# Adaptive layer norm, S4 convolution and a 2048x2048 FFN on one core: the first two row blocks convolved without their shift, and an impulse response from two frequency blocks

## The chip, the cores and the metric

The kernel runs on one core of one Trainium2 chip. The metric is the device time of one execution in microseconds (us), the median of several runs. The engines are TensorE (PE in the profile; PEld is its weight load), VectorE (DVE), ScalarE (ACT), GpSimd (POOL) and SyncE (SP); SP, and in a few places ScalarE, issue the DMA transfers.

## The reference, cut to what matters

The input `x` has 4 batches of 1024 rows with 2048 positions. A vector `c` per batch is multiplied with `wmod` and gives six modulation vectors for each batch: `sa, ca, ga` (shift, scale, gate) for the convolution, `sb, cb, gb` for the FFN.

```python
mod = (silu(c) @ wmod).reshape(4, 6, 1, -1)
h = layernorm(x) * (1 + ca) + sa
x = x + ga * s4(h)            # y = causal convolution of h with K along the row, + D*h
h = layernorm(x) * (1 + cb) + sb
x = x + gb * (h @ W.T + bias + low-rank update)
```

`K` is the impulse response of a state space model with 64 states: a rational function (`at_roots`) is evaluated at 2048 frequencies and brought back by an inverse Fourier transform. The convolution is linear: the convolution of `n*(1+ca) + sa` is that of `n*(1+ca)` plus that of `sa`, and the latter is one vector for all rows of a batch.

## The kernel before, in words

**Rows.** The 4096 rows are 32 row blocks of 128 ("row 0" to "row 31" below), eight to a batch. Each is a tile of 128x2048 f32.

**Modulation.** `wmod` is 100 MB of f32, read as six *sections* of 16 *chunks* of 1 MB each. `section` loads a chunk (`mod_load`, on SP's queue, L313) and multiplies it (`mod_mm`, L318: four matmuls with column tiling, each of two passes, so x8 in the trace) into one PSUM bank. The order is sections 1 (`ca`), 0 (`sa`), 2 (gate `ga`), 4, 3, 5. Sections 1 and 0 alternate between two pools of three chunk buffers each, later ones have three. After a section, `mod_column` copies the bank to `mrow`, transposes it (`mtp`) and keeps it as columns; `fold_scale` takes the largest value over the partitions (an all-reduce on GpSimd), makes a power of two of it and scales `ca` and `sa`. For section 2 `mod_gate` builds the gate on VectorE and ScalarE, and `gate_tile` spreads it over the partitions by four matmuls `gps` (L628) into `gat` (L629).

**Impulse response.** `toeplitz` is a generator; the list `KT` says after which chunks of sections 1 and 0 it goes a step further. `s4` spreads cosines and sines over the partitions by matmuls (`s4cs`, L153) for four blocks of 512 frequencies; both halves of the 128 partitions hold the 64 states (the lower half computes the real part, the upper the imaginary part). Each block takes some five elementwise steps of 128x512 and a reciprocal on VectorE (L163 to L171) and 4 matmuls `s4rp` (L178). Then follow small steps on 128x16, the transform (`s4kp`), the maximum, a store of the response to DRAM (`kd`, L257) and a load of it as 128 shifted copies (`kb`, L261, 1 MB, on ScalarE's queue). Four matmuls with an anti-diagonal matrix (`kbps`, L265) turn `kb` round, and VectorE makes six f16 filter tiles of it (`kh0..2`, `kl0..2`; high and low parts, L282 to L286).

**Convolution of a row.** `conv_load`, `stats` (L498 to L500), `normalize` (L515). `conv_prep` transposes the row in four groups of four (`tp`, L536, in two PSUM buffers of the pool `tps`), ScalarE applies scale and shift (`t`, L539), and both it and VectorE split the result in f16 halves (`hc`, `hs`, L545 to L548). `conv_mm` runs three families of f16 matmuls (L568) into the banks `ya` and `yb` of the pool `acc` (five banks, shared with `lps` and the FFN). Between the families it calls `tick`, which advances other work. ScalarE copies `ya` (`qs`, L581), VectorE adds `yb` to it (L585); with `early=False` VectorE also multiplies with the gate and adds `x` with row sums (L587 to L595). With `early=True`, for rows 0 and 1, that is left to `conv_late` (L604, L605), after the gate exists. `conv_post` stores the row to `x1d` and prepares the second layer norm; only after it can the buffer of `x` be loaded with the row four further on.

**Weights of the FFN.** From row 3 on (`R0`), `step` advances the generator `fill`: `prep_lora` loads `A` (`la`, L390) and `Bf` (`lb`, L403), both 2 MB in the same buffer (tag `we`), scales them, takes an all-reduced maximum and splits `lb` in `lbh` (ScalarE, L419) and `lbl` (VectorE, L420). `merge` then computes for eight column blocks products `lps` (L444, six matmuls to a PSUM bank) that VectorE adds to the weights `we` (L446), and stores the results. The rest of the time, after row 31, is the FFN itself (L704).

**Order.** The program is written in the order of `net`; a scheduler of the framework fixes the order of the instructions on each engine when the kernel is built, by data, buffers and priorities. On the chip each engine takes its list in that order. The names `s4cs`, `s4rp`, `kbps`, `tp`, `gps`, `lps` are tiles in the trace.

Of the kernel before, what the change touches and what calls it, by code (L numbers as in the profile page):

```python
# [24 lines left out]
P = 128  # L25
# [9 lines left out]
class Net:  # L35
# [40 lines left out]
    def s4(self, pool):  # L76
# [12 lines left out]
        cs = T([3, 2, D], "s4cs", BF16)  # L89
        nc.scalar.dma_start(out=cs, in_=io["t_cs"])  # L90
        one = T([3, P], "s4one", BF16)
        v.memset(one, 1.0)
# [30 lines left out]
        coef = T([P, 8], "s4coef")  # L123
        t8 = T([P, 8], "s4t8")
        lo, hi = slice(0, 64), slice(64, 128)
        lam, pv, qv, ct = (vec[:, i, :] for i in range(4))
        for i, (x, y) in enumerate(((ct, bq), (ct, pv), (qv, bq), (qv, pv))):
            re, im = t8[:, 2 * i : 2 * i + 1], t8[:, 2 * i + 1 : 2 * i + 2]
            tt(re, x[:, 0:1], y[:, 0:1], MUL)
            stt(re, x[:, 1:2], y[:, 1:2], re, MUL, ADD)  # L130
            tt(im, x[:, 1:2], y[:, 0:1], MUL)
            stt(im, x[:, 0:1], y[:, 1:2], im, MUL, SUB)
        t8v = t8.rearrange("p (v c) -> p v c", c=2)
        cov = coef.rearrange("p (v c) -> p v c", c=2)
        v.tensor_copy(coef[lo], t8[lo])
        tsc(cov[hi, :, 0], t8v[hi, :, 1], -1.0, None, MUL)
        v.tensor_copy(cov[hi, :, 1], t8v[hi, :, 0])
# [3 lines left out]
        fa = T([P, 2], "s4fa")  # L141
        v.tensor_copy(fa[lo, 0:1], nl[lo, 0:1])
        v.tensor_copy(fa[hi, 0:1], lam[hi, 1:2])
        v.memset(fa[lo, 1:2], 0.0)
        tsc(fa[hi, 1:2], ts2[hi], -1.0, None, MUL)
        rp = self.tps.tile([P, 16, 8], F32, tag="t", name="s4rp")
        w = 512
        cps = {}

        def table(c0):  # L150
            cps[c0] = [self.acc.tile([P, w], F32, tag="a", name="s4cs") for _ in range(2)]
            for i, ps in enumerate(cps[c0]):
                nc.tensor.matmul(ps, one, cs[:, i, ds(c0, w)], start=True, stop=True)  # L153

        yield
        table(0)
        table(w)
        for c0 in range(0, D, w):
            cc, sc = cps[c0]
            wi = pool.tile([P, w], F32, tag="s4wi", name="s4wi", bufs=2)  # L160
            wr = pool.tile([P, w], F32, tag="s4wr", name="s4wr", bufs=2)
            nu = pool.tile([P, w], F32, tag="s4nu", name="s4nu", bufs=2)
            tsc(wi, sc, ts2, None, MUL)  # L163
            stt(wi, cc, nl[:, 1:2], wi, MUL, ADD)
            nc.scalar.activation(wr, cc, AF.Square, scale=nl[:, 0:1])
            tsc(nu, sc, fa[:, 1:2], None, MUL)
            stt(nu, cc, fa[:, 0:1], nu, MUL, ADD)
            nc.scalar.activation(wi, wi, AF.Square)
            tt(wr, wr, wi, ADD)
            v.reciprocal(wr, wr)  # L170
            tt(nu, nu, wr, MUL)  # L171
            if c0 < 2 * w:
                yield
                table(c0 + 2 * w)
            yield
            for c in range(w // P):
                g = c0 // P + c
                nc.tensor.matmul(  # L178
                    rp[:, g, :], nu[:, ds(P * c, P)], coef,
                    start=(g == 0), stop=(g == NC - 1), skip_group_check=True,  # L180
                )
# [54 lines left out]
    def toeplitz(self, pool):  # L236
# [24 lines left out]
        nc.scalar.dma_start(out=kb, in_=src)  # L261
        yield
# [8 lines left out]
        self.kf = []  # L271
        for f in range(3):
# [5 lines left out]
            else:  # L278
                src = pool.tile([P, HC, P], F32, tag="kdif", name="kdif")
# [7 lines left out]
            self.kf.append((hi, lo))  # L287
# [77 lines left out]
    def fold_scale(self, pool, mul, add, name, winv=None):  # L365
# [9 lines left out]
        s, inv = self.pow2(self.cst, self.allmax(pool, m, NB, name), NB, name)  # L375
        for t in (mul, add):
            v.tensor_tensor(t, t, s.unsqueeze(1).to_broadcast([P, NC, NB]), MUL)  # L377
        return inv


    def prep_lora(self, pool, tmp):
# [21 lines left out]
        nc.sync.dma_start(out=b, in_=io["BfT"].rearrange("(k p) o -> p k o", p=P))  # L403
# [21 lines left out]
    def merge(self, pool, tmp, c):  # L425
        nc, v = self.nc, self.nc.vector
        lf = tmp.tile([P, 2, 2, P], F32, tag="laf", name="laf")
# [95 lines left out]
    def conv_prep(self, pl, r, x, st, out):  # L523
# [8 lines left out]
        for c0 in range(0, NC, 4):  # L532
# [4 lines left out]
            for k in range(4):  # L537
                c = c0 + k
                nc.scalar.activation(  # L539
                    t[:, k], tp[:, k], AF.Identity,  # L540
                    bias=self.sa[:, c, b : b + 1], scale=self.ca[:, c, b : b + 1],
                )
# [56 lines left out]
    def conv_late(self, x, y, sums):  # L599

        v = self.nc.vector
        for q in range(2):
            sl = ds(1024 * q, 1024)
            v.tensor_tensor(y[:, sl], y[:, sl], self.gat[:, sl], MUL)  # L604
# [164 lines left out]
WM, WMS = 3, 3  # L769
X0 = (20, 26)  # L770
LEFT0 = 30
KT = (0, 3, 5, 6, 8, 11, 14, 18, 24)
# [11 lines left out]
def net(ctx: ExitStack, tc: tile.TileContext, io):  # L784
# [40 lines left out]
    for name in ("lora", "mrg"):  # L825
        pl[name] = pool(right, "p1" + name, 1, "right")

# [12 lines left out]
    pl["sm"] = pool(left, "p1sm", 4)  # L840
    st = ExitStack()
    toe = k.toeplitz(pool(st, "st", 1))
    wms = pool(st, "wms", WMS)
# [3 lines left out]
    xs, hs = {}, {}  # L847
    sts = {}
    n = 0
    for sec in (1, 0):  # L850
        for _ in section(sec, (wms, wmp)):
            if n in KT:
                with tc.issue_after(k.last.ins), tc.high_priority():
                    take(toe, 1)
            if n in X0:
                r = X0.index(n)
                xs[r] = k.conv_load(pl, r)
# [209 lines left out]
```

## Time and profile before

| | us |
|---|---|
| median of 3 runs (2142.97 to 2143.06) | 2143.01 |
| the profiled execution | 2143.54 |
| its span, first to last instruction | 2141.7 |
| TensorE busy in the span | 2076.2 (97%) |
| VectorE, ScalarE busy | 1321.9 (62%), 928.7 (43%) |
| DMA moved | 483.06 MB, 226 GB/s on average |
| the two costliest groups: FFN matmuls L704 (5376), convolution matmuls L568 (3456) | 1198, 953 |

Mean granted clock of TensorE: 0.984 of full speed. In the profile a line is read as: place in the program, engine, operation, output tile from input tiles, shape, count, and in brackets the idle time of that engine just before it with the instruction or transfer that ended it. Matmuls are pipelined, so durations of single matmuls overlap; counts and start times are the better guide there.

### The profile page before, as it was taken

How to read it: one execution, taken by the hardware profiler on the slowest of the kernel's cores; microseconds unless marked ns; L12 is line 12 of the kernel's file. 1: busy time of each engine (PE TensorE's matmuls, PEld its weight loads, DVE VectorE, ACT ScalarE, POOL GpSimd, SP SyncE). 2: the span in 40 equal slices, each digit the busy share in tenths (PEclk: the TensorE clock that was granted, in tenths of full speed). 3: DMA queues.
4: the chain of work that ended last, by engine and by line, in shares of the span. 5: the costliest groups of instructions: out<-in, count | busy, mean ns of one | idle time of the engine just before them, and what ended most of it. 6: DMA issues, size and time to landing. Idle time of an engine off the chain costs nothing.

```text
span 2141.7 us, 28401 instructions
## 1 busy us (share of the span) xinstructions
PE 2076.2 (97%) x11084; PEld 1020.2 (48%) x11084; DVE 1321.9 (62%) x2357; ACT 928.7 (43%) x1699; POOL 3.3 (0%) x12
## 2 busy tenths in 40 slices
PE   7698999999999999999999999999999999999998
PEld 2144555455455555554545545545444444444444
DVE  7449889888899998665565565565533333332323
ACT  1148667666677766755454454555200000000000
POOL 0000000000000000000000000000000000000000
PEclk8799999999999999999999999999999999999999
DMA  9988578767875553387565565564794545455542
GB/s 401 377 297 312 190 295 300 269 245 274 315 297 180 185 190 117 133 347 262 182 241 187 194 228 193 203 236 176 272 354 160 189 155 171 163 162 168 175 158 70
DMA packets 127137, 483.06 MB, mean 226 GB/s; under 512 B 13670, under 2 KB 13799, under 8 KB 96023
## 3 DMA queue, kind: packets, MB, share of 16 engines
q1 hardware_dynamic: 126464, 479.65, 61.8%
q8 instruction: 87, 1.43, 0.3%
q10 hardware_dynamic: 538, 1.59, 0.2%
q14 instruction: 48, 0.39, 0.1%
HBM read 325.89 MB, written 155.30 MB: 225 GB/s over the span
## 4 chain that ended last, share of the span: by engine, by line
PE 73%; DVE 12%; ACT 5%; DMA 3%; issue 1%; SPq 0%; DVEq 0%; ACTq 0%
PE fZ L704 22%; PE fY L704 15%; PE fX L704 15%; PE ya L568 9%; PE yb L568 5%; PE tp L654 2%; PE lps L444 2%; PE modps L318 2%; DVE y L595 1%; ACT x L614 1%; ACT t L539 1%; PE tp L536 1%; DVE hc L548 1%; DVE st L498 1%; DVE y L594 1%
## 5 line engine op out<-in xcount | busy, mean ns | idle before, releaser
L704 PEld LDWEIGHTS <-lf 128*128 128x128 f16 x5376 | 526.0, 98 | 620.8 <-issue 1.1
L704 PE MATMUL fZ<-w,lf 128*128 128x512 f16 x2304 | 513.6, 379 | 0.8 <-ACT p L712 0.8
L704 PE MATMUL fX<-w,lf 128*128 128x512 f16 x1536 | 342.8, 379 | 0.0
L704 PE MATMUL fY<-w,lf 128*128 128x512 f16 x1536 | 342.0, 379 | 0.0
L568 PEld LDWEIGHTS <-hc 128*128 128x128 f16 x2304 | 214.5, 98 | 203.3 <-issue 40.6
L722 DVE TENSOR_TENSOR xo<-xo,gb 128x512 f32<-128x512 f32 x128 | 87.8, 690 | 241.8 <-DMA xo<-x1d 229.1
L539 ACT ACTIVATE t<-tp,sa,ca 128x128 f32<-128x128 f32 x512 | 202.5, 476 | 13.3 <-DVE sa L377 5.1
L568 PE MATMUL ya<-kh,hc 128*128 128x512 f16 (+3 forms) x768 | 191.7, 327 | 4.0 <-ACT qs L581 3.9
L568 PE MATMUL ya<-kh,hs 128*128 128x512 f16 (+3 forms) x768 | 194.1, 328 | 0.7 <-DVE hs L548 0.7
L568 PE MATMUL yb<-kh,hc 128*128 128x512 f16 (+3 forms) x768 | 190.9, 326 | 0.0
L712 ACT COPY p<-fZ 128x512 f32<-128x512 f32 x64 | 37.3, 583 | 285.6 <-PE fZ L704 271.9
L712 ACT COPY p<-fX 128x512 f32<-128x512 f32 x32 | 18.8, 587 | 316.3 <-PE fX L704 241.2
L568 PEld LDWEIGHTS <-hs 128*128 128x128 f16 x1152 | 107.7, 98 | 98.1 <-issue 18.3
L656 ACT ACTIVATE gt<-tp,sb,cb 128x256 f32<-128x256 f32 x256 | 125.6, 579 | 60.5 <-PE tp L654 60.5
L318 PE MATMUL modps<-wm,sct 128*32 128x512 f32 x768 | 121.6, 692 | 23.9 <-DMA wm<-in_wmod 15.3
L568 PE MATMUL ya<-kl,hs 128*128 128x512 f16 (+3 forms) x384 | 125.6, 327 | 0.0
L568 PE MATMUL ya<-kl,hc 128*128 128x512 f16 (+3 forms) x384 | 125.6, 327 | 0.0
L568 PE MATMUL yb<-kl,hc 128*128 128x512 f16 (+3 forms) x384 | 125.1, 326 | 0.0
L727 DVE TENSOR_TENSOR fin<-fX,gb 128x512 f32<-128x512 f32 x32 | 22.1, 692 | 128.2 <-PE fX L704 128.1
L536 PE MATMUL tp<-ident,n 128*128 128x128 f32 x512 | 80.6, 282 | 17.2 <-ACT t L539 13.8
L548 DVE TENSOR_TENSOR hc<-t,hc 128x512 f16<-128x512 f32 x128 | 87.6, 684 | 5.6 <-ACT hc L547 5.6
L444 PE MATMUL lps<-lbh,lac 128*128 128x512 f16 x256 | 85.0, 380 | 0.6 <-ACT lbh L419 0.6
(241 smaller groups left out, 2211.4 us busy)
## 6 DMA issues: line engine op xcount, KB each, us to landing
wm<-in_wmod SPq DMA_DIRECT2D x96, 1024.0 KB, 7.3
lfd<-lf SPq DMA_DIRECT2D x112, 512.0 KB, 3.2
lf<-lfd SPq DMA_DIRECT2D x112, 512.0 KB, 3.8
x<-in_x SPq DMA_DIRECT2D x32, 1024.0 KB, 5.6
x1d<-y SPq DMA_DIRECT2D x32, 1024.0 KB, 5.2
x<-x1d SPq DMA_DIRECT2D x32, 1024.0 KB, 5.6
xo<-x1d SPq DMA_DIRECT2D x128, 256.0 KB, 3.8
out<-xo SPq DMA_DIRECT2D x128, 256.0 KB, 3.3
```

What stands on the lines that cost most here:

```text
L318: self.last = self.nc.tensor.matmul(self.modps[32 * g : 32 * g + 32, :], self.sct[:, j].rearrange("p r b -> p (r b)"), w[:, ds(512 * g, 512)],
L444: nc.tensor.matmul(ps, la[:, x, k, h], y[:, k, osl], start=(n == 0), stop=(n == 5))
L536: nc.tensor.transpose(tp[:, k], n[:, ds(P * (c0 + k), P)], self.ident)
L539: nc.scalar.activation(t[:, k], tp[:, k], AF.Identity, bias=self.sa[:, c, b : b + 1], scale=self.ca[:, c, b : b + 1],)
L548: v.tensor_tensor(lo[:, sl], src, hi[:, sl], SUB)
L568: nc.tensor.matmul(pf[:, o:512], h, self.kf[f][z][:, ds(k0, 512 - o)], start=first, stop=(i == last and (x, z) == (1, 0)), skip_group_chec ...
L654: nc.tensor.transpose(tp[:, c, r], xs[r][:, ds(P * (c0 + c), P)], self.ident)
L656: nc.scalar.activation(t[:, c0 + c], tp[:, c], AF.Identity, bias=self.sb[:, c0 + c, b : b + 1], scale=self.cb[:, c0 + c, b : b + 1],)
L704: nc.tensor.matmul(ps[name], lf[i][:, k, x, :], wc[i][k // 4][:, k % 4, y, :], start=(first and n == 0), stop=(n == 3 * HC - 1), skip_grou ...
L712: nc.scalar.copy(t, ps[name])
L722: v.tensor_tensor(x, x, self.gbias[:, h], ADD)
L727: v.tensor_tensor(t, cv, self.gbt[:, h], MUL)
```

## The change

There are three parts.

1. *Impulse response.* The partitions' halves now hold the same states at different frequencies (0 to 1023 in the lower, 1024 to 2047 in the upper). The table has six rows in place of three, and the matrix that spreads it comes with it from DRAM. There are two blocks of 512 columns in place of four; the real and the imaginary part of each summand are both kept, and two `s4rp` matmuls per 128 columns, with coefficients that are zero for the other half, take the place of one. The six filters are made in the order 0, 2, 1, and `kb` is kept for `shift_conv`.
2. *Rows 0 and 1 without the shift.* `early_scale` makes a scale `es` from `ca` of batch 0 alone, when section 1 is done. Rows 0 and 1 are prepared with it and without `sa`, and convolved between the chunks of section 0 (`row` advances that section from `conv_mm`). When `sa` is known, `shift_conv` convolves it by 16 small f32 matmuls (`gsp`), and `shift_add` spreads the result over the partitions by 16 f32 matmuls (`gsb`) and adds it to both rows (eight adds on VectorE). `conv_late` multiplies these rows by the ratio of the two scales.
3. *The order around it.* Row 2 is convolved early as well (`EARLY = 3`), between section 2's chunks; the loop starts at row 3. The row pools are opened ahead of the impulse response, which with its chunk pool (two buffers, `WMS`) goes to the other side of the memory; the pools of `prep_lora` and `merge` are opened after it is closed. `lb` is loaded on ScalarE's queue; `laf` has two buffers.

The diff, cut to its core:

```diff
-        cs = T([3, 2, D], "s4cs", BF16)
-        nc.scalar.dma_start(out=cs, in_=io["t_cs"])
-        one = T([3, P], "s4one", BF16)
-        v.memset(one, 1.0)
+        ct = T([6, D + P], "s4cs", BF16)
+        nc.scalar.dma_start(out=ct, in_=io["t_cs"])
+        cs = ct[:, 0:D].rearrange("p (i n) -> p i n", i=2)
+        one = ct[:, D:]
...
-        def table(c0):
-            cps[c0] = [self.acc.tile([P, w], F32, tag="a", name="s4cs") for _ in range(2)]
-            for i, ps in enumerate(cps[c0]):
-                nc.tensor.matmul(ps, one, cs[:, i, ds(c0, w)], start=True, stop=True)
...
+        cps = [[self.acc.tile([P, w], F32, tag="a", name="s4cs") for _ in range(2)] for _ in range(2)]
+        for n in range(2):
+            for i, ps in enumerate(cps[n]):
+                nc.tensor.matmul(ps, one, cs[:, i, ds(n * w, w)], start=True, stop=True)
+
+        def tiles(name):
+            return [pool.tile([P, w], F32, tag=name, name=name, bufs=2) for _ in range(2)]
+
+
+        wi, wr = tiles("s4wi"), tiles("s4wr")
+        wq = pool.tile([P, 2, w], F32, tag="kdif", name="s4wq")
+        wq = [wq[:, n] for n in range(2)]
+        for n, (cc, sc) in enumerate(cps):
+            tsc(wi[n], sc, ts2, None, MUL)
+            stt(wi[n], cc, nl[:, 1:2], wi[n], MUL, ADD)
+            nc.scalar.activation(wr[n], cc, AF.Square, scale=nl[:, 0:1])
+            nc.scalar.activation(wq[n], wi[n], AF.Square)
+        for n, (cc, sc) in enumerate(cps):
+            tt(wq[n], wr[n], wq[n], ADD)
+            v.reciprocal(wq[n], wq[n])
+            stt(wr[n], cc, nl[:, 0:1], wq[n], MUL, MUL)
+            tt(wi[n], wi[n], wq[n], MUL)
             yield
             for c in range(w // P):
-                g = c0 // P + c
-                nc.tensor.matmul(
-                    rp[:, g, :], nu[:, ds(P * c, P)], coef,
-                    start=(g == 0), stop=(g == NC - 1), skip_group_check=True,
-                )
+                out = rp.rearrange("p (h g) v -> p g h v", h=2)[:, 4 * n + c]
+                for i, x in enumerate((wr[n], wi[n])):
+                    nc.tensor.matmul(
+                        out, x[:, ds(P * c, P)], cf[:, i],
+                        start=(n, c, i) == (0, 0, 0), stop=(n, c, i) == (1, 3, 1), skip_group_check=True,
+                    )
...
-        for f in range(3):
+        self.kf = {}
+        for f in (0, 2, 1):
...
-        s, inv = self.pow2(self.cst, self.allmax(pool, m, NB, name), NB, name)
+        self.hs, inv = s, _ = self.pow2(self.cst, self.allmax(pool, m, NB, name), NB, name)
...
+    def early_scale(self, pool):
+        v = self.nc.vector
+        m = pool.tile([P, 1], F32, tag="esm", name="esm")
+        v.tensor_reduce(m, self.ca[:, :, 0], AX.X, ALU.max, apply_absolute_value=True)
+        v.tensor_scalar(m, m, LNMAX, None, MUL)
+        self.es, self.einv = self.pow2(self.cst, self.allmax(pool, m, 1, "es"), 1, "es")
+        self.cae = self.kpool.tile([P, NC], F32, tag="cae", name="cae")
+        v.tensor_scalar(self.cae, self.ca[:, :, 0], self.es, None, MUL)
+
+    def shift_conv(self, pool):
+
+        nc, v = self.nc, self.nc.vector
+        sa = pool.tile([P, NC], F32, tag="sae", name="sae")
+        v.tensor_scalar(sa, self.sa[:, :, 0], self.es, self.hinv[:, 0:1], MUL, MUL)
+        ps = self.tps.tile([P, NC], F32, tag="t", name="gsp")
+        for m in range(NC):
+            nc.tensor.matmul(
+                ps[:, m:NC], self.kb[:, ds(P * m, P)], sa[:, 0 : NC - m],
+                start=(m == 0), stop=(m == NC - 1), skip_group_check=True,
+            )
+        self.gsc = self.kpool.tile([P, NC], F32, tag="gsc", name="gsc")
+        v.tensor_copy(self.gsc, ps)
+
+    def shift_add(self, ys):
+        nc, v = self.nc, self.nc.vector
+        for q in range(4):
+            ps = self.tps.tile([P, 4, P], F32, tag="t", name="gsb")
+            for c in range(4):
+                nc.tensor.matmul(
+                    ps[:, c], self.gsc[:, 4 * q + c : 4 * q + c + 1].to_broadcast([P, P]), self.ident,
+                    start=(c == 0), stop=(c == 3), skip_group_check=True,
+                )
+            for y in ys:
+                sl = ds(512 * q, 512)
+                v.tensor_tensor(y[:, sl], y[:, sl], ps.rearrange("p c t -> p (c t)"), ADD)
...
-        nc.sync.dma_start(out=b, in_=io["BfT"].rearrange("(k p) o -> p k o", p=P))
+        nc.scalar.dma_start(out=b, in_=io["BfT"].rearrange("(k p) o -> p k o", p=P))
...
-        lf = tmp.tile([P, 2, 2, P], F32, tag="laf", name="laf")
+        lf = tmp.tile([P, 2, 2, P], F32, tag="laf", name="laf", bufs=2)
...
+                if shift:
+                    nc.scalar.activation(
+                        t[:, k], tp[:, k], AF.Identity,
+                        bias=self.sa[:, c, b : b + 1], scale=self.ca[:, c, b : b + 1],
+                    )
+                else:
+                    nc.scalar.activation(t[:, k], tp[:, k], AF.Copy, scale=self.cae[:, c : c + 1])
...
-            v.tensor_tensor(y[:, sl], y[:, sl], self.gat[:, sl], MUL)
+            v.scalar_tensor_tensor(y[:, sl], y[:, sl], ratio, self.gat[:, sl], MUL, MUL)
...
-WM, WMS = 3, 3
-X0 = (20, 26)
+WM, WMS = 3, 2
+EARLY = 3
+X0 = 11
 LEFT0 = 30
-KT = (0, 3, 5, 6, 8, 11, 14, 18, 24)
+KT = (0, 5, 7, 11)
...
+    for name, bufs in (("h", 2), ("n", 1), ("t", 2), ("y", EARLY), ("g", 1)):
+        pl[name] = pool(left, "p1" + name, bufs)
     st = ExitStack()
-    toe = k.toeplitz(pool(st, "st", 1))
-    wms = pool(st, "wms", WMS)
+    toe = k.toeplitz(pool(st, "st", 1, "right"))
+    wms = pool(st, "wms", WMS, "right")
...
-    for sec in (1, 0):
-        for _ in section(sec, (wms, wmp)):
-            if n in KT:
-                with tc.issue_after(k.last.ins), tc.high_priority():
-                    take(toe, 1)
-            if n in X0:
-                r = X0.index(n)
-                xs[r] = k.conv_load(pl, r)
-                sts[r] = k.stats(pl, xs[r], "1")
-            n += 1
-    xs[2] = k.conv_load(pl, 2)
+    for _ in section(1, (wms, wmp)):
+        if n in KT:
+            with tc.issue_after(k.last.ins), tc.high_priority():
+                take(toe, 1)
+        if n == X0:
+            load(0)
+        n += 1
+    k.early_scale(msm)
+    load(1)
+    sec = section(0, (wms, wmp))
+    for r in range(2):
+        stats(r)
+        take(prep(r, False), 9)
+    take(sec, 1)
+    with tc.issue_after(k.last.ins), tc.high_priority():
+        take(toe, 2)
+    take(sec, 1)
+
+    def row():
+        take(sec, 1)
+
+    for r in range(2):
+        ys[r] = k.conv_mm(pl, hs.pop(r), xs[r], row, True)
+        load(r + 2)
+    take(sec, 17)
+    k.shift_conv(msm)
+    k.shift_add([ys[r][0] for r in range(2)])
     st.close()
...
+    for name in ("lora", "mrg"):
+        pl[name] = pool(right, "p1" + name, 1, "right")
...
     sec = section(2, (wmp,))
-    take(prep(0), 9)
-    take(prep(1), 9)
-    stats(2)
-    take(sec, 16)
-    load(3)
-    ys = {0: k.conv_mm(pl, hs.pop(0), xs[0], lambda: None, True)}
+    for r in range(2, EARLY + 1):
+        stats(r)
     take(prep(2), 9)
-    stats(3)
-    ys[1] = k.conv_mm(pl, hs.pop(1), xs[1], lambda: None, True)
+    ys[2] = k.conv_mm(pl, hs.pop(2), xs[2], row, True)
     nxt = prep(3)
+    take(nxt, 9)
+    take(sec, 17)
+    k.gat = k.gate_tile(pl["g"], 0)
+    ratio = k.kpool.tile([P, 1], F32, tag="rat", name="rat")
+    nc.vector.tensor_tensor(ratio, k.einv, k.hs[:, 0:1], MUL)
+    for r in range(EARLY):
+        k.conv_late(xs[r], *ys[r], ratio if r < 2 else 1.0)
+        k.conv_post(pl, r, xs.pop(r), *ys[r])
+        if r < 2:
+            load(r + 4)
+    stats(EARLY + 1)
+    nxt = prep(EARLY + 1)
     take(nxt, 1)
-    take(sec, 1)
-    k.gat = k.gate_tile(pl["g"], 0)
-    for r in range(2):
-        k.conv_late(xs[r], *ys[r])
-        k.conv_post(pl, r, xs.pop(r), *ys[r])
     post = None
-    for r in range(2, 32):
-        if r + 2 < 32:
+    for r in range(EARLY, 32):
+        if EARLY + 2 < r + 2 < 32:
```

## The prediction, made before the changed kernel ran

> **What bounds the kernel now.** I read the page first: TensorE (PE) has work for 97% of the span, so a gain must come from the 65 us in which it has none, or from the stretches in which it runs at a low clock. Then I asked for the busy time by stretch, cut where TensorE's behaviour changes; columns are busy us and instructions of each engine, granted TensorE clock, DMA share, GB/s.
>
> ```profile
> PE 2076.2 (97%) x11084; PEld 1020.2 (48%) x11084; DVE 1321.9 (62%) x2357; ACT 928.7 (43%) x1699; POOL 3.3 (0%) x12
> ```
>
> ```profile
> 8.59:97.70 89.11, 65.75 (x320) 18.69 (x321) 53.77 (x110) 8.88 (x15) 0.95 (x3) 0.74 1.01 421
> 97.70:105.50 7.80, 4.99 (x18) 1.78 (x16) 5.55 (x17) 4.45 (x12) 0.41 (x1) 0.72 0.45 188
> 105.50:162.50 57.00, 57.00 (x375) 24.95 (x373) 26.79 (x56) 27.83 (x71) 0.00 (x0) 1.00 0.85 294
> 162.50:207.50 45.00, 36.36 (x216) 19.15 (x214) 42.17 (x102) 40.18 (x69) 1.05 (x1) 0.93 0.85 330
> 207.50:300.00 92.50, 90.90 (x546) 47.02 (x545) 80.29 (x160) 63.05 (x132) 0.00 (x0) 1.00 0.65 245
> ```
>
> There are four regimes. Until 97.7 us the DMA is full (421 GB/s): the modulation weights of sections 1 and 0 set the pace, 2.49 us for each 1 MB chunk, and TensorE waits at clock 0.74. From 105.5 to 162.5 TensorE never stops (rows 0 and 1 with section 2's chunks). From 162.5 to 207.5 VectorE (DVE) is 94% busy and TensorE loses 8.6 us. After 207.5 TensorE is full again. So rows 0 and 1 can be moved into the first regime; the third is where it may be given back.
>
> The third regime in the timeline (start, duration, engine, line; in brackets idle time and what ended it). TensorE's rows first, then VectorE's:
>
> ```profile
> 196.83 1.09 PE L536 MATMUL tp<-ident,n 128*128 128x128 f32 x8 [1.56 <-DVE n L515]
> 199.18 0.66 PE L536 MATMUL tp<-ident,n 128*128 128x128 f32 x4 [1.26 <-ACT t L539]
> 201.41 1.12 PE L536 MATMUL tp<-ident,n 128*128 128x128 f32 x4 [1.57 <-ACT t L539]
> 204.58 1.91 PE L318 MATMUL modps<-wm,sct 128*32 128x512 f32 x2 [2.05 <-DMA wm<-in_wmod]
> 207.10 0.58 PE L444 MATMUL lps<-lbh,lac 128*128 128x512 f16 x1 [0.60 <-ACT lbh L419]
> 207.48 0.63 PE L568 MATMUL ya<-kh,hs 128*128 128x512 f16 x1
> ```
>
> ```profile
> 163.65 1.67 DVE L629 TENSOR_SCALAR gat<-gps,fs_i,ks_i 128x512 f32<-128x512 f32 x2 [0.80 <-PE gps L628]
> 165.35 1.23 DVE L604 TENSOR_TENSOR y<-y,gat 128x1024 f32<-128x1024 f32 x1
> 195.44 1.33 DVE L515 TENSOR_SCALAR n<-x,mv,rs 128x2048 f32<-128x2048 f32 x1
> ```
>
> The gate tile is there at 163.65; behind it on VectorE stand the late work of rows 0 and 1, and row 4's normalisation follows only at 195.44, 31.8 us later. TensorE lives meanwhile on the convolutions of rows 2 and 3 (35 us). Row 4's convolution starts at 207.5. I call this moment **row 4's entry** and compare the kernels there, since the work behind it is the same.
>
> **What the skill says.** "TensorE: Matmul & The Clock Gate", section "HAM oscillation — how this bites in real kernels", states that waits for DMA between short bursts throw the array back to half clock. The trace agrees: a chunk's eight matmul passes take 1.94 us in the first regime and 1.06 us from 107 us on. I use 1.94 until TensorE runs without pause and 1.06 after. "DMA: Bandwidth & Descriptors", section "Issuing engines are not separate DMA queues", says that a transfer issued by another engine shares the same DMA engines, so moving `lb` to ScalarE's queue buys no bandwidth; in the trace, `kb` on that queue needs 9.5 us for 1 MB while SP's weights stream.
>
> **Part 1, the impulse response.** Two frequency blocks in place of four: VectorE saves 2 x 3.34 us of reciprocals and two blocks of five or so 512-wide steps (0.65 to 0.75), 14 us. In the built order the last `s4rp` matmuls stand behind chunk 8, which arrives at 26 us: done at 28.3, plus 16 passes of 0.155 us (`s4rp` before: 8 in 1.24) makes 31 (before 48.5). From there 9.3 us to the store of `kd` (48.5 to 57.8 before) and 16.2 until `kb` lands (57.8 to 74.0): 57 us, 17 earlier.
> But `kbps` now stands behind other things on TensorE. The section 1 chunks end at 50.5 (chunk 12 at 36, then x0 and four chunks at 2.49, then 1.94); copy and transposes 2.1; the new early scale with its all-reduce 4.3 (`fold_scale`'s chain before takes 3.8, from 97.1 to 100.9); four `t` of ScalarE 1.6 that free the PSUM buffer; a transpose group 1.1; three quarters of a chunk 1.5: 61.2. Then 6.6 to the last copy of `kb` (73.97 to 80.57 before) and 10.1 for the six filters on VectorE (79.9 to 90.0): **TensorE runs without pause from 78 us**, with 21 chunks and 4.3 us of row 0 done, where before it did from 105.5.
>
> **Part 2, TensorE's work from 78 to the end of section 2.** A row is 41,472 columns at 0.216 us per 512: 17.5 us. Rest of rows 0 and 1 30.7, row 2 17.5, row 3's share in the built order 4.9; 27 chunks at 1.08 29.2; 48 transposes at 0.125 and the column's four 6.5; `shift_conv` 32 passes (between 0.13, the transposes, and 0.155, `s4rp`) 4.5; `shift_add` 32 passes at 0.13 4.1. Sum 97.4: 175.4. Waits in the built order: normalisation of row 1 0.5; gsp, copy, gsb, adds through two PSUM buffers 1.8 (eight adds at 0.6 on an idle VectorE); row 2's preparation now starts only after that, 1.5; row 3's transposes behind ScalarE 2; the last chunks through three buffers 1. I take 6.5 (3 to 12): **section 2 ends at 182** (154.4 before, but with a row and a half less behind it).
>
> **Part 3, the end of the early stage.** `prep_lora` is now followed closely. `la` is issued behind section 0 (117) and is harmless. ScalarE squares it within row 2's preparation and issues `lb` at about 152; 9.1 us to land (the row before; 5 to 19 by `kb` and `la`); scalings, row 3's preparation (11), the sums, the all-reduce and the second scaling put the first `lbh` at about 185 to 188. The first `lps` matmul, right behind section 2's last chunk, waits for it: 3 us (0 to 6), and row 3's convolution and the gate matmuls `gps` are queued behind that. The gate's absolute value on ScalarE also stands behind `lbh` (before at once, 155.2). With 7 us of matmuls and the two `lbl` of VectorE (2.25 each) between, **the gate tile starts at 192**.
> From there VectorE's built order to row 4's normalisation is: gate 3.2; 12 late steps for three rows at 1.15 (165.35 and on, start to start) 13.9; row 3's evacuation 3; six statistics 3.7; one `we` 0.7; two dozen small steps 2.9; the normalisation 1.3: 28.7. Transposes, `t`, casts 3: row 4's entry at **223.8**. In these 32 us TensorE has only 8.4 us of row 3, `gps` 2, four chunks 4.1 and 24 `lps` 5.2, the last behind PSUM banks that VectorE frees late.
>
> **The sum.** Before, entry at 207.5. Ahead of its entry the changed kernel has done 29 more `lps` (6.3), three quarters of a chunk more (0.8) and four transposes fewer (0.5): 6.6. So 223.8 - 207.5 - 6.6 = +9.7 us. The profiled execution took 2143.54 (span 2141.7 and 1.8 around it), 0.5 over the median of the runs: 2143.0 + 9.7 = **2152.7**. Hidden at no cost: the ratio in `conv_late` (same step), the f order, `laf`'s second buffer, two more x loads early (DMA is free after 78), s4's extra copies.
>
> **Rivals.** (1) *Faster, 2132.* Counted without VectorE's queue: TensorE starts 27.5 us earlier; since then it has extra 11 chunks 11.9, gsp and gsb 8.6, the column 0.5, minus 4.3 of row 0 and 0.2 transposes: 16.5. Gain 11, if its waits from there to 300 us stay at the 10.2 of before (8.6 and 1.6). For: in the first regime TensorE was idle or slow for over 40 us, and VectorE is nearly idle until 160. Against: three late rows hang on one gate, with one row to cover them in place of two. It decides from a gate tile at 182 or earlier. (2) *No change, 2143:* both halves meet; the gate at about 182 to 187, less idle behind it. (3) *Worse, 2161:* `lb` takes the 18 us of `la`, ScalarE waits with row 3's preparation behind it, +8. That the response isn't ready earlier (so the change misses its aim) ends here too: each us at 78 is a us at the end.
>
> **Numbers.** Forecast 0.53 (own range 2147.5 to 2158), rival 1 0.21, rival 2 0.14, rival 3 0.12. A measurement tells 0.2% (4.3 us) from no change: faster 0.21, same 0.14, slower 0.65. The range leaves out the outer halves of rivals 1 and 3 (0.17): 2131 to 2161.
>
> **What would show it.** In the profile after: `kb` landing near 57 and `kbps` near 61; PE share over 95% from 78 us; section 2's last chunk near 182; the first gate row on VectorE near 192; row 4's normalisation 27 to 30 us behind it, with TensorE idle for over 8 us just ahead, waiting on DVE `n` and `we`. I am wrong if the gate comes before 184, or if TensorE finds work in that stretch.

## The result, and the profile after

The changed kernel takes 2149.16 us (median of 8 runs, 2146.49 to 2152.91) beside 2142.84 (8 runs, 2141.51 to 2144.57) of the kernel before: ratio 1.003, interval 1.0019 to 1.004. It is 6 us slower. The profiled execution took 2149.26, its span 2147.5 (before 2143.54 and 2141.7).

First the line of busy time, from the page of the changed kernel:

```profile
PE 2085.0 (97%) x11144; PEld 1028.0 (48%) x11144; DVE 1313.8 (61%) x2356; ACT 922.0 (43%) x1697; POOL 3.0 (0%) x13
```

TensorE is busy 8.8 us longer and idle 3.0 us less (62.5 for 65.5): 5.8 us of span. Now the busy time by stretch of the changed kernel (columns as in the prediction):

```profile
8.59:50.00 41.41, 32.13 (x164) 11.57 (x160) 23.66 (x65) 2.30 (x4) 0.95 (x3) 0.75 0.99 405
...
60.00:69.00 9.00, 8.33 (x37) 2.85 (x32) 7.93 (x13) 6.53 (x20) 0.00 (x0) 1.00 0.97 403
69.00:130.00 61.00, 61.00 (x397) 29.80 (x394) 26.77 (x64) 13.52 (x36) 0.41 (x1) 0.97 0.77 293
130.00:180.00 50.00, 44.75 (x310) 19.83 (x302) 20.70 (x47) 33.32 (x71) 0.35 (x1) 1.00 0.84 321
180.00:200.00 20.00, 16.96 (x63) 5.70 (x60) 10.90 (x11) 8.57 (x6) 0.00 (x0) 0.75 0.80 290
200.00:230.00 30.00, 23.27 (x118) 10.26 (x117) 29.63 (x68) 12.71 (x26) 0.00 (x0) 0.83 0.87 330
230.00:300.00 70.00, 65.35 (x388) 33.55 (x387) 65.79 (x144) 54.13 (x115) 0.00 (x0) 0.98 0.70 250
```

The first regime ends at 69 us in place of 105.5: that is the aim of the change, and it is met. From 130 to 300 TensorE then loses 19.7 us, and from 180 to 230 its clock falls to 0.75 and 0.83 as well. The same stretches as single rows, TensorE's in the timeline of the changed kernel:

```profile
60.69 3.70 PE L263 MATMUL kbps<-kb,rev 128*128 128x512 f32 x8
68.65 0.38 PE L608 MATMUL ya<-kl,hs 128*128 128x512 f16 x1 [0.67 <-DVE kl L285]
...
185.70 0.58 PE L481 MATMUL lps<-lbh,lac 128*128 128x512 f16 x1 [2.10 <-ACT lbh L456]
...
213.03 0.38 PE L481 MATMUL lps<-lbh,lac 128*128 128x512 f16 x1 [2.54 <-DVE y L625]
...
218.45 0.59 PE L481 MATMUL lps<-lbh,lac 128*128 128x512 f16 x1 [3.35 <-DVE y L634]
...
227.52 0.38 PE L608 MATMUL ya<-kh,hs 128*128 128x512 f16 x1
```

And VectorE's, with the gate tile, the first late step and row 4's normalisation:

```profile
195.47 1.67 DVE L669 TENSOR_SCALAR gat<-gps,fs_i,ks_i 128x512 f32<-128x512 f32 x2 [3.90 <-PE gps L668]
197.18 1.28 DVE L644 SCALAR_TENSOR_TENSOR y<-y,rat,gat 128x1024 f32<-128x1024 f32 x1
...
222.04 1.33 DVE L552 TENSOR_SCALAR n<-x,mv,rs 128x2048 f32<-128x2048 f32 x1
```

The picture is the forecast one: the gate is late (195.5), row 4's normalisation is 26.6 us behind it, and the `lps` matmuls in between wait for PSUM banks that VectorE frees late (`y`). Row 4's convolution begins at 227.5.

**Where row 4 really begins in the kernel before.** The prediction took the `ya<-kh,hs` row at 207.48 for row 4. The convolution matmuls behind that point, and behind 228.10 (stretch, busy us and count, weight loads, clock, DMA share, GB/s):

```profile
207.40:2142.00 1934.60, 538.23 (x3096) 288.23 (x3095) 1.00 0.59 212
228.10:2142.00 1913.90, 524.45 (x3024) 281.37 (x3023) 1.00 0.60 213
```

28 rows of 108 are 3024. The 72 more belong to row 3: a row is worked in two halves of its output, the first of 36 matmuls and the second of 72, and 207.48 is the start of row 3's second half. Row 4 begins at 228.17. For the same reason the "rows 2 and 3 (35 us)" that the prediction has ahead of 207.48 are row 2 and a third of row 3 (144 matmuls, 23.7 us busy), and row 4's normalisation at 195.44 had 20.7 us of row 3 behind it as cover. From row 4's start to the first FFN matmul (L704, L744) the two kernels have nearly the same work. First the kernel before, its stretch and two groups of matmuls in it (count, busy us, mean ns, idle us just before):

```profile
228.10:920.25 692.15, 678.76 (x4210) 366.32 (x4208) 613.97 (x1277) 487.73 (x1008) 0.38 (x1) 1.00 0.63 234
```

```profile
L444 PE MATMUL lps<-lbh,lac 128*128 128x512 f16 x237 | 78.6, 379 | 0.0
L318 PE MATMUL modps<-wm,sct 128*32 128x512 f32 x358 | 48.5, 611 | 0.0
```

Then the changed kernel:

```profile
227.50:927.65 700.15, 680.07 (x4206) 366.12 (x4206) 624.17 (x1304) 492.18 (x1028) 0.41 (x1) 1.00 0.62 230
```

```profile
L481 PE MATMUL lps<-lbh,lac 128*128 128x512 f16 x237 | 78.7, 379 | 0.4 <-DVE we L483 0.4
L317 PE MATMUL modps<-wm,sct 128*32 128x512 f32 x352 | 49.4, 606 | 4.6 <-DMA wm<-in_wmod 4.6
```

237 `lps` on both sides, 358 and 352 passes of chunks. The six passes are under 1 us. So an account can be made in two parts, from TensorE's busy time in each trace (matmuls of one kind that overlap are counted once):

| from the start of the unbroken run to row 4 | us |
|---|---|
| start, 68.9 for 105.5 | -36.6 |
| chunks still to do: 264 passes (40.2 us) for 149 (21.8) | +18.4 |
| `gsp` 3.7, `gsb` 5.2 | +8.9 |
| the column's four `mtp` 0.6, fewer `tp` -1.8 | -1.2 |
| the same 30 `lps` (10.8 for 7.5) and four rows (77.6 for 76.0), longer at the low clock | +4.9 |
| idle 15.0 for 9.8 | +5.2 |
| sum -0.4; measured, 227.5 for 228.2 | -0.7 |
| **from row 4 to the FFN**, 700.2 for 692.2: idle 20.1 for 13.4, busy +1.3 | +8.0 |
| **FFN to the end**, 1219.8 for 1221.4 | -1.6 |
| span, sum | +5.7 |

A lead of 36.6 us is worth nothing at row 4: 26 of it is work that was moved or added, 10 is waits and low clock. Behind row 4 come 8 more, the largest single one 4.6 at 278 us, where a chunk isn't there.

### The profile page after: what moved, and what is told of

It is laid out like the page before. It is cut to its first block, busy times and chain, and to the rows that moved or that the text cites. A ratio compares the mean times of both kernels' runs of the same rounds, so it can differ in the third digit from the quotient of the medians.

```text
span 2147.5 us, 28491 instructions
## 1 busy us (share of the span) xinstructions
PE 2085.0 (97%) x11144; PEld 1028.0 (48%) x11144; DVE 1313.8 (61%) x2356; ACT 922.0 (43%) x1697; POOL 3.0 (0%) x13
## 4 chain that ended last, share of the span: by engine, by line
PE 59%; DVE 6%; DMA 2%; ACT 2%; issue 1%; SPq 0%; DVEq 0%; ACTq 0%
PE fZ L744 23%; PE fY L744 15%; PE fX L744 15%; PE ya L608 3%; PE tp L694 2%; PE yb L608 1%; DVE y L635 1%; DMA xo<-x1d 1%; ACT x L654 1%; DVE wch L509 1%; DVE hc L588 1%; DVE st L535 1%; DMA w<-wcd 1%; ACT t L577 1%; DVE y L634 0%
## 5 line engine op out<-in xcount | busy, mean ns | idle before, releaser
L744 PEld LDWEIGHTS <-lf 128*128 128x128 f16 x5376 | 526.0, 98 | 620.5 <-issue 0.9
L744 PE MATMUL fZ<-w,lf 128*128 128x512 f16 x2304 | 514.1, 379 | 0.6 <-ACT p L752 0.6
L744 PE MATMUL fX<-w,lf 128*128 128x512 f16 x1536 | 342.1, 379 | 0.0
L744 PE MATMUL fY<-w,lf 128*128 128x512 f16 x1536 | 342.1, 379 | 0.0
L577 ACT ACTIVATE t<-tp,sa,ca 128x128 f32<-128x128 f32 x480 | 189.3, 474 | 20.2 <-PE tp L573 19.9
L696 ACT ACTIVATE gt<-tp,sb,cb 128x256 f32<-128x256 f32 x256 | 125.0, 576 | 62.5 <-PE tp L694 60.9
```

Of the source, the lines that this page charges most:

```text
L577: nc.scalar.activation(t[:, k], tp[:, k], AF.Identity, bias=self.sa[:, c, b : b + 1], scale=self.ca[:, c, b : b + 1],)
L696: nc.scalar.activation(t[:, c0 + c], tp[:, c], AF.Identity, bias=self.sb[:, c0 + c, b : b + 1], scale=self.cb[:, c0 + c, b : b + 1],)
L744: nc.tensor.matmul(ps[name], lf[i][:, k, x, :], wc[i][k // 4][:, k % 4, y, :], start=(first and n == 0), stop=(n == 3 * HC - 1), skip_grou ...
```

## The experiments

Two theories stood at the start. **The gate** (mine): the loss is made of waits between the gate tile and row 4, and of the low clock that follows from them; VectorE's queue sets them. **The matmuls**: it is the price of `gsp` and `gsb`. A third, **the lora chain**, is the `la`, `lb`, `lbh` work of `prep_lora`, which stands in the in-order queues. Each ratio is to the kernel before, timed beside that run (its medians lay between 2143.1 and 2145.6, so that ratios compare better than times); the changed kernel has 1.003.

| run | us | ratio, interval |
|---|---|---|
| e1_response_only | 2155.7 | 1.0059 (1.0046 to 1.0071) |
| e2_response_later | 2159.9 | 1.0076 (1.0062 to 1.0091) |
| e3_no_shift | 2148.7 | 1.0021 (1.0013 to 1.0028) |
| e4_lora_later | 2150.6 | 1.0033 (1.0022 to 1.0044) |
| e5_late_spread | 2154.9 | 1.0036 (1.0023 to 1.0049) |
| e6_chunks_ahead | 2161.6 | 1.0073 (1.0060 to 1.0085) |
| e7_gate_early | 2164.5 | 1.0082 (1.0069 to 1.0095) |
| e8_gate_early_lora_later | 2151.3 | 1.0027 (1.0020 to 1.0035) |
| e9_cover | 2167.9 | 1.0111 (1.0095 to 1.0126) |
| e10_before_cover | 2167.0 | 1.0102 (1.0088 to 1.0116) |
| e11_response_retimed | 2145.4 | 1.0002 (0.9993 to 1.0010) |
| e12_cover_lora_ahead | 2130.2 | 0.9936 (0.9922 to 0.9949) |

**1 and 11. The response alone.** To the kernel before, `s4`, `toeplitz` and `tables` of the changed one; run 11 also

```diff
-KT = (0, 3, 5, 6, 8, 11, 14, 18, 24)
+KT = (0, 5, 7, 11, 20, 21)
```

> The kernel before with the impulse-response part alone (two blocks of 512 frequencies, filters in the order 0, 2, 1); order of rows and sections as before. If TensorE's start is set by the weights of sections 1 and 0 (my theory), the response is ready some 15 us earlier but nothing waits for it: 2143, within 1.5 us of the kernel before. If the response paces the start of the rows, TensorE's unbroken run starts up to 15 us earlier: 2128 to 2135.

> The kernel before with the impulse-response part alone, as in the first experiment, but with the last two steps (kbps and the filters) taken behind chunks 20 and 21 in place of an early chunk at which TensorE waited 13 us for kb, with the chunk buffers full and the weights' stream down to 63 GB/s. If that wait was the 12 us that the first experiment lost: 2143 to 2145, as before, since the rows start behind section 0. If the response in two blocks costs by itself (more matmuls, other queues): still above 2150.

Run 1 was 12 us slower, which neither theory had. With the old list the steps come too early: `kbps` stands on TensorE ahead of chunks that are there, and waits. From run 1, the row of TensorE and the stretch around it:

```profile
54.03 5.63 PE L263 MATMUL kbps<-kb,rev 128*128 128x512 f32 x8 [13.01 <-DMA kb<-kd]
```

```profile
50.00:60.00 10.00, 5.97 (x12) 2.39 (x16) 1.00 (x2) 1.17 (x2) 0.00 (x0) 0.60 0.15 63
```

While TensorE waits, no chunk buffer comes free, and the weights' stream, 422 GB/s at the start of this run, falls to 63. In the kernel before the same 10 us have 422, so there is no spare rate to catch up with. Run 11, which moves the later steps as well, takes the wait away: no difference from before. So the response alone is worth nothing and costs nothing, as long as TensorE isn't made to wait for it.

**2. The response later.** In the changed kernel `KT = (3, 8, 10, 14)` for `(0, 5, 7, 11)`.

> The changed kernel with the steps of the impulse response taken three section-1 chunks later (7.5 us at 2.49 us for a chunk). If each us at the start of TensorE's unbroken run (68.9 us) is a us at the end, kb lands at 68 instead of 60.6, the run starts at about 76, and the time is 2149 + 7 = 2156 (2154 to 2157). If the stage is bound by the transfers anyway and the chunks catch up later, 2149 to 2151.

`kbps` at 66.0 for 60.7, the gate tile at 204.7 for 195.5, and 9.9 us by the ratios (0.0046 of 2143). The first case, and more than it: the early response is needed once the rows are moved.

**3. Without the shift.** `shift_conv` and `shift_add` are not called.

> The changed kernel without the convolution of the shift and its addition to rows 0 and 1 (that part of the result is left out). If the loss is the price of the added matmuls: 8.9 us of TensorE and about 1.8 of waits around them go, 2149 - 10.7 = 2138.5. If the stretch between the gate and row 4 sets the time, and section 2's last chunks come at the pace of the transfers (DMA share 0.84 there), the gate moves up by less, by 4 to 7: 2142 to 2145, with the idle time ahead of row 4 as long as it was or longer.

Neither time came. The gate tile is 4 us earlier (191.5), as the second case had it, but the time can't be told from that of the changed kernel. TensorE, with 8.9 us less to do, is idle for 11.6 us from 140 to 180 in place of 4.9: it waits there for section 2's chunks (7.6 us) and for `t` of ScalarE (3.9), and after 180 for VectorE to empty the chunks' bank (`mg`, 4.5). From 180 to 230 it is idle for 9.8 us, as in the changed kernel. The matmuls theory falls: their time was cover for other waits.

**4. The lora chain a row later.** `R0 = 4` for `3`.

> The changed kernel with the FFN weights' work (prep_lora, merge) begun one row later, at row 4. If the lbh chain on ScalarE ahead of the gate is what costs the time, the gate comes 3 to 5 us earlier and the time falls by as much: 2144 to 2146. If the 27 us of VectorE between gate and row 4's normalisation set the time (my theory), the gate's gain is small, and row 3's convolution now stands ahead of the gate and the 24 lps matmuls are gone from behind it, so that TensorE has less to cover the stretch with: idle time ahead of row 4 grows by 5 to 10, 2149 + 5 = 2154 (2150 to 2159).

The gate tile came 4 us earlier and the time didn't fall (+0.7 us by the ratios, within the intervals). As foreseen the cover behind the gate is gone; on TensorE:

```profile
220.26 1.97 PE L573 MATMUL tp<-ident,n 128*128 128x128 f32 x8 [14.82 <-DVE n L552]
```

**5. The late work spread.** The core of the edit:

```diff
-    for r in range(EARLY):
-        k.conv_late(xs[r], *ys[r], ratio if r < 2 else 1.0)
...
+    lated(0)
     stats(EARLY + 1)
     nxt = prep(EARLY + 1)
     take(nxt, 1)
+    todo = {(3, 1): 1, (3, 4): 2}    # lated(1), lated(2) in row 3's ticks
```

> The changed kernel with the late work of rows 1 and 2 taken behind row 4's statistics and normalisation (row 0's stays right behind the gate). If VectorE's queue between gate and row 4's normalisation sets the time (my theory): eight late steps of 1.15 us leave the queue, row 4's load and small steps remain, normalisation 6 to 9 us earlier than 222, row 4's entry near 219: 2149 - 6 = 2143 (2141 to 2146). If the loss lies in the added matmuls or in the lbh chain ahead of the gate: no change, 2148 to 2150.

A miss: no gain. In the built order row 4's statistics still follow most of the late work, since they have to wait for `x4`, which takes the buffer of row 0 (late work, `conv_post` on ScalarE, then the load). Its rows on VectorE, and the next wait on TensorE:

```profile
215.31 2.47 DVE L535 BATCH_NORM_STATS2 st<-x 128x6 f32<-128x512 f32 x4 [0.98 <-DMA x<-in_x]
...
223.95 1.33 DVE L552 TENSOR_SCALAR n<-x,mv,rs 128x2048 f32<-128x2048 f32 x1
```

```profile
224.44 1.92 PE L317 MATMUL modps<-wm,sct 128*32 128x512 f32 x2 [7.99 <-DMA wm<-in_wmod]
```

So VectorE's queue isn't the bound by itself, as my theory had it; the chain through the x buffer is as long, and SP's queue, in which chunks of section 4 stand behind x loads that wait for that buffer, takes over.

**6, 7 and 8. The gate earlier.** Run 6 takes chunks of sections 0 and 2 at 2, 2, 1 to a tick. Run 7 takes them at 2 and 1 in turn, holds each convolution group behind the last chunk, makes the gate tile within row 2, and puts row 3's preparation and the late work of rows 0 and 1 there. Run 8 is run 7 with `R0 = 4`. The core of run 7:

```diff
+    sec = chain(section(0, (wms, wmp)), gated())    # run 6: section(2)
     def row():
-        take(sec, 1)
+        take(sec, next(pat))
```

> The changed kernel with the chunks of sections 0 and 2 taken faster (2, 2, 1 to a tick, section 2 beginning within row 1), so that in the built order all of section 2 and the gate's matmuls stand ahead of nearly all of row 3's convolution (before, some 11 us of row 3 stood behind the gate; now 17). If the cover behind the gate sets the time: the gate tile some 8 us earlier, 6 us more to cover with, 2149 - 7 = 2142 (2138 to 2145). If it is the added matmuls or TensorE waits for the chunks as for those of sections 1 and 0, no change or worse, 2149 to 2153.

> The changed kernel with the convolutions of rows 0 to 2 held behind the chunks (2 and 1 to a tick, in turn, the gate tile made at once within row 2), row 3's preparation and the late work of rows 0 and 1 within row 2's convolution, late work of row 2 ahead of row 4's statistics. By my theory the gate comes near 160 with over 25 us of convolutions behind it, no pause ahead of row 4, so no half clock either: 10 us of idle time and 8 of low clock saved less waits for chunks of 5: 2149 - 13 = 2136 (2132 to 2141). If the added matmuls are the loss, the time stays above 2145; if TensorE waits for chunks all along, above 2149.

> As the early-gate kernel, and prep_lora and merge begun one row later, at row 4. With the gate early there is cover behind it either way; VectorE has less to do around row 4. By my theory the same within 3 us or a little better, 2134 (2130 to 2140). If the lbh chain matters in itself, 4 us better than the early-gate kernel; if the matmuls of lps are needed as cover, 3 to 8 us worse than it.

The gate tile came at 182.9, 175.1 and 173.7, up to 22 us earlier, and none of the three was faster; runs 6 and 7 lost 9 and 11 us to the changed kernel. In run 6 TensorE waits from 60 us on 9.0 us for chunks, 11.0 for row 4's `n` and 3.7 for `lbh`. In run 7 the gate's steps on VectorE stand behind a product of two tiny tiles of `prep_lora`; VectorE's row, then TensorE's:

```profile
171.41 0.16 DVE L437 TENSOR_TENSOR lwt<-lws 128x2 f32<-128x2 f32 x1 [5.58 <-DMA lws<-in_scales]
```

```profile
173.03 3.78 PE L673 MATMUL gps<-mg,ident 128*128 128x512 f32 x4 [4.82 <-DVE mg L348]
```

Later it waits 13.7 for section 4's chunks and 8.1 for `t` of ScalarE. Run 8 moves only `prep_lora` and `merge` and regains 11.8 us (0.0055 of 2143), three times what was expected if the chain mattered. This made the lora chain the first suspect, though `lps`, which goes with it, was moved as well.

**9 and 10. Cover.** Rows 4 and 5 have x buffers of their own, in memory that `prep_lora` takes from row 6 on; row 4 is ready ahead of the gate; the late work lies in rows 3 and 4. Run 10 is the same on the kernel before.

```diff
+    pl["ext"] = pool(stx, "p1ext", 1, "right")    # x4, x5, y of row 3
-R0 = 3
+R0 = 6
+    lates = {(3, 4): 0, (3, 7): 1, (4, 1): 2}     # lated(r) in these ticks
```

> The changed kernel up to the gate, then another order: rows 4 and 5 are loaded early into buffers of their own (in the memory that prep_lora and merge take later; these begin at row 6), row 3's result has its own buffer too, row 4 is prepared ahead of the gate, and the late work of rows 0 to 2 is spread over the convolutions of rows 3 and 4. If the loss is made of the waits from the gate to row 4 (x4 has to wait for row 0's late work, la and lb stand in the queues and in section 2's transfers) and of the half clock that follows from them: 9.8 us idle from 180 to 230, 4.6 at 278 and 8 of low clock go, less some new waits: 2149 - 18 = 2131 (2127 to 2138). If the loss is the added matmuls: 2147 to 2150. If the delayed weights of section 4 and of the FFN are missed later: 2140 to 2147.

> The kernel before with the same treatment (rows 4 and 5 early in buffers of their own, row 2's result in one, late work of rows 0 and 1 spread over row 2, prep_lora and merge from row 6). It had 8.6 us idle and some 3 of low clock in that stretch: 2143 - 10 = 2133 (2130 to 2138). If the first stage of the changed kernel is worth what the ledger says (start 36.6 us earlier, less 14.7 of chunks and 8.9 of shift matmuls: 13, less 5 of waits before 180), the changed kernel with the same treatment is 3 to 8 us faster than this one; if the early start is worth nothing, it is equal or slower.

Both were 22 to 24 us slower than before. Yet the stretch aimed at was mended; the changed kernel with cover, by stretch:

```profile
180.00:200.00 20.00, 19.73 (x112) 10.05 (x110) 15.55 (x27) 10.49 (x26) 0.00 (x0) 1.00 0.36 140
200.00:230.00 30.00, 29.56 (x179) 15.53 (x177) 30.00 (x71) 19.89 (x40) 0.00 (x0) 1.00 0.84 317
...
260.00:300.00 40.00, 16.11 (x80) 4.60 (x81) 13.32 (x42) 21.77 (x35) 0.35 (x1) 0.64 0.87 337
```

From 180 to 230 only 0.7 us are lost, at full clock (before the cover 9.8). But now there is a hole from 256 to 300, where `prep_lora` stands. Its rows on ScalarE, on VectorE and on TensorE:

```profile
284.59 3.89 ACT L443 ACTIVATE lb<-lb,lwt 128x2048 f32<-128x2048 f32 x2 [9.50 <-DMA lb<-in_BfT]
```

```profile
260.99 0.16 DVE L436 TENSOR_TENSOR lwt<-lws 128x2 f32<-128x2 f32 x1 [4.37 <-DMA lws<-in_scales]
...
292.67 0.43 DVE L585 TENSOR_TENSOR sm<-t 128x256 f32<-128x256 f32 x1 [17.48 <-ACT t L577]
```

```profile
268.10 1.94 PE L573 MATMUL tp<-ident,n 128*128 128x128 f32 x8 [12.19 <-DVE r_v L69]
...
292.69 1.11 PE L573 MATMUL tp<-ident,n 128*128 128x128 f32 x4 [4.91 <-ACT t L577]
```

TensorE waits for a row's preparation twice. The longer wait (12.2 us, to 268.1) starts on VectorE: the tiny product of run 7 waits 4.4 us for `lws` again, and the row's statistics and normalisation stand behind it. For the later one, read from below: `t` stands on ScalarE behind the scaling of `lb`; that waits for a transfer of 2 MB, which could be issued only when the squares of `la` were done, since both use one buffer (issued 271.2, 13.4 us to the scaling). Between the two TensorE has only chunks to do and waits for them (8.4 us). The trace agrees with the Trainium skill, "PSUM — Partial Sum Buffer", section "Engine vs sequencer instructions", by which VectorE's and ScalarE's queues are strictly first in, first out. Runs 9 and 10 end within 0.9 us of each other. By the expectation of run 10 that is the case of an early start worth nothing. But both come to the same chain at row 6 (row 6's first `qs` at 247.1 and 249.3; run 10 waits 3.7 us for `lws` and 4.7 for `lb`), and the 2.2 us that run 9 is ahead there are gone at the end.

**12. The lora chain taken apart.** Run 9 with `prep_lora` in pieces; its core:

```diff
-        b = tmp.tile([P, 2, D], F32, tag="we", name="lb")
-        nc.scalar.dma_start(out=b, in_=...)
+        b = tmp.tile([P, 2, D], F32, tag="lb", name="lb")    # own buffer
+        nc.sync.dma_start(out=b, in_=...)                    # right behind la
+        for _ in range(9):
+            yield                                            # a row later
...
+            with self.tc.issue_after(self.qsi.ins):          # behind that row's qs
                 nc.scalar.activation(av[:, k], ...)          # a yield after each piece
...
+        with self.tc.issue_after(self.yi.ins):               # behind that row's y on VectorE
             v.tensor_tensor(wt, ws[:, 0, :], ws[:, 1, :], MUL)   # lwt
```

> The changed kernel with the cover of the ninth experiment, and prep_lora taken apart: la and lb are loaded together into buffers of their own at row 6, and their squares, scales and splits follow a row later, a piece per tick, behind that row's qs on ScalarE. In the ninth experiment TensorE lost 32 us from 260 to 400 while ScalarE waited for la (2.7) and lb (9.5) with the preparation of row 8 behind them. If prep_lora's waits on the in-order queues are what costs the time, wherever it stands: nearly all of that and its half clock go, 2168 - 35 = 2133 (2128 to 2140), faster than both kernels. If it is its work on ScalarE (19.5 us of passes) or the missing of section 4's weights: 2145 to 2160.

2130.16 us, 38 less than run 9 and faster than both kernels: 13.7 us less than before (0.0064 of 2143). Row 4's first `qs` is at 197.9 (231.5 before), the FFN begins at 906.4 (920.3). Its line of busy time and the same stretch:

```profile
PE 2076.9 (98%) x11144; PEld 1024.4 (48%) x11144; DVE 1309.0 (62%) x2356; ACT 924.5 (43%) x1697; POOL 3.4 (0%) x13
```

```profile
260.00:300.00 40.00, 38.40 (x248) 21.29 (x247) 32.84 (x82) 33.38 (x69) 0.00 (x0) 1.00 0.60 223
```

ScalarE's work is the same (924.5 us, 924.0 in run 9); its waits for `la` (2.7) and `lb` (9.5) and VectorE's for `lws` (4.4) are gone. So it was the waits, not the 19.5 us of passes. How much each of the edits gave wasn't split. Nor is this the loss of the changed kernel itself, which waits neither for `lb` nor for `lws`: both waits come with `prep_lora` at row 6, in runs 9 and 10.

## Why the prediction was right, and where it was wrong

The time (2149.2 for 2152.7), the sign and the place of the first waits came out. The sum that led there did not: errors of opposite sign made it, so that the time is right by luck. From the forecast +9.7 us, the wrong landmark takes 14.1, row 4's late entry adds 3.7, the work behind it 8.0, and the FFN takes 1.6: +5.7, where the spans differ by 5.8.

- **Start of the unbroken run, 78: it was 68.9.** `kb` landed near 60.6, 3.6 later than I had it, and `kbps` came at 60.69 (61.2 forecast). But the clock was full from 60 on (1.00), so `kbps` took 3.70 us; and row 0 needs only the first pair of filters (TensorE's only wait is 0.67 for `kl`, at 68.65), not the 10.1 us of all six. The two terms were mis-sized by 9 us.
- **Section 2's end, 182: it was 183.6**, from a run begun 9 us earlier. The waits were as forecast (6.2 us for 6.5), but TensorE was busy for 108.5 us, not 97.4. By 68.9 it had done less than I had it do by 78 (19 chunks for 21, and under 1 us of row 0 for 4.3), which is about 6 of the 11 us; and a pass of a chunk took 0.15 us on the average, where I had 0.135. So most of the 9 us was work put off, not time won.
- **`lbh`, 3 us: 2.1. The gate tile, 192: 195.5** (a part of `gps` at the low clock, behind the rows in the built order). **28.7 us of VectorE: 26.6**, with `lps` waiting for banks, as foreseen: 5.9 us on `y` and 0.5 on `we`, where I had over 8 on `n` and `we`. **Row 4's entry, 223.8: 227.5.**
- **"Row 4's convolution starts at 207.5": this step failed.** It was row 3's second half, which then covered the wait for row 4 in the kernel before. With the true 228.2 and equal work behind it, my own terms give 223.8 - 228.2 = -4.4, about 2139, which is between the rivals of no change and of faster. Measured is -0.7.
- **"The work behind it is the same", so nothing is lost behind it: wrong by 8.0 us.** The work is the same, the waits are not. 4.6 of it is the chunk at 278; run 2 has the same wait, run 5 one of 2.6. It wasn't taken away by itself, and stays open.
- **The rivals.** The early start of 36.6 us could not be worth more than 10 or 11 here, since 26 of them are the chunks and the shift's matmuls; waits and clock took the rest. Rival 1's condition, a gate by 182, was met in runs 7 and 8 and wasn't enough: it had left out the x buffer (run 5) and the lora chain. Rival 3's mechanism, ScalarE waiting for `lb` with a row's preparation behind it, is not in the changed kernel, where `lb` was issued at 147.9 and scaled at 160.1 without a wait; it is in run 9, as one part of the 38 us that run 12 regains.

Open is what the change is worth where nothing gives it back, and so how much of run 12's 13.7 us is the change's: the kernel before with both measures, cover and lora taken apart, wasn't run. Runs 9 and 10 show no difference, but both stand at the same chain.

## What to carry to other kernels

Before two kernels are compared at a landmark, count the instructions that are left behind it: one label was wrong by 72 of a row's 108 matmuls here, and the forecast by 14 us. Work that is moved forward has to be paid out in a place without waits; here each mended wait uncovered the next in-order queue (VectorE, then the x buffer and SP, then VectorE at `lws` and ScalarE at `lb`), and only with the last mended did the kernel become faster. In an in-order queue, load a tile a stage ahead into its own buffer and place its use late, however little the use costs.

## What the runs showed of the hardware

- In the changed kernel TensorE's clock was full (1.00) from 60 to 69 us, with the DMA still at 403 GB/s. The prediction had half clock for this whole stage, by the Trainium skill, "TensorE: Matmul & The Clock Gate", section "HAM oscillation — how this bites in real kernels". The rule that this section starts from is about idle gaps of over some 3.4 us. Of the eleven waits for chunks in the kernel before, from 8.59 to 97.7 us, ten were 0.5 to 1.7 us long and one 3.5, and the clock doesn't go by their length. Two chunks of the kernel before, and a stretch of the changed one in which TensorE was busy throughout at half clock:

```profile
85.81 1.06 PE L318 MATMUL modps<-wm,sct 128*32 128x512 f32 x8 [1.42 <-DMA wm<-in_wmod]
...
90.78 1.93 PE L318 MATMUL modps<-wm,sct 128*32 128x512 f32 x8 [0.80 <-DMA wm<-in_wmod]
```

```profile
30.00:40.00 10.00, 10.00 (x52) 4.87 (x48) 5.65 (x38) 0.00 (x0) 0.00 (x0) 0.52 0.99 398
```

  What sets the clock in this stage is not shown here. The same eight `kbps` passes took 3.70 us in the changed kernel and 5.63 in run 1, behind a wait of 13 us.
- One wait of 13 us on TensorE in a stage bound by the DMA cost 12 us of the whole: the stream all but stopped with the chunk buffers full (63 GB/s for 10 us).
- A product of two 128x2 tiles (0.16 us) held VectorE for 5.6, 4.4 and 3.7 us in runs 7, 9 and 10, each time for a transfer of 0.5 KB; in run 9 its two loads of `in_scales` were issued at 249.9 and 250.6 and the product ran at 261.0.
